# Decoding neighbour counts two per 16 bit word, with weights stored by parity of node

## The chip, the cores and the metric

The kernel runs on one core of a Trainium2 chip. The metric is the device time of the whole launch in microseconds (us). Before the change it is 418.17 us, the median of three runs (416.35 to 418.49). One further run was profiled; it is told of below.

## The reference

Two graph layers are computed over 3327 nodes with 64 features each and a symmetric 0/1 adjacency matrix `adj`. Layer 0 is attention in hyperbolic space: for every pair of nodes (i, j) with an edge, a sigmoid of two projections, times a logarithmic map of the pair, summed over j. Layer 1 is a weighted sum whose weights decay by rank:

```python
h = relu(layernorm(x));  x = x + layer0(h, adj)
h = relu(layernorm(x))
support = h @ weight
rank = cumsum(adj != 0, axis=1); deg = rank[:, -1:]; k = minimum(deg, 100.0)
pos = rank - (deg - k)
w = mask * where(pos > 0, 0.5 ** (k - pos), 0)
x = x + w @ support + bias
```

For a node i, the last neighbour in the order of j has the weight 1, the one before it 1/2, and so on, for at most 100 neighbours. So the weight of an edge (i, j) is fixed by how many neighbours of i stand behind j. That number, the count, fits in 8 bits. A 16 bit pattern that holds the count shifted left by seven places is, read as bf16, a power of two; the kernel uses this to turn counts into weights with a multiplication by 128.

## The kernel before, in words

The 3327 nodes are padded to 26 blocks of 128 (`NB`, 3328 columns, `NP`). The columns, which are the nodes i, are cut into four strips of 8, 8, 6 and 4 blocks (`STRIPS`). For each strip the blocks of nodes j (on the partitions) are walked from 25 down to 0 in rounds; a round holds up to 1024 columns.

In each round of the main loop (L1209) the adjacency tile comes by DMA (`ad`), ScalarE makes tanh (L653) and two Gelus (L857, L858) of products that TensorE has made (L670, L671), VectorE multiplies (L658, L663), and TensorE adds the result up over j (`po`, L680). Beside this, and for layer 1 only, VectorE makes a mask of the edges (L620), TensorE accumulates the counts in PSUM (`pc`, L631 and L632), and `read` takes the counts of one j out of PSUM with a clip at zero. It runs on ScalarE (L642) or VectorE (L644, L646); `ON_ACT` says in what share. 22 of the 26 blocks j are kept as 8 bit counts (`behind_lo`, `behind_hi`). Four blocks, `JD` = 12 to 15, are kept at once as 16 bit weights (`weight_of`), by a factor of 128 in the same read; there are 4 blocks by 4 strips = 16 such reads.

Layer 1 comes at the end. `order` lists the blocks j: first the four of `JD`, then 0 to 11 and 16 to 21; blocks 22 to 25 (`late`) come last, as their features are ready last. For each block that isn't in `JD`, `decode` turns its 3328 counts into a 16 bit tile `wt` of 3328 weights (7 buffers): the first, third and so on of the 22 on ScalarE (L1285), the others on VectorE (L1287). A decode is issued `LEAD` = 4 blocks ahead of its use. TensorE then adds seven products per block (L1299), one per chunk of 512 columns (the last has 256), into seven PSUM tiles `pw`.

Between the decodes stands another chain. The result of layer 0 for the last strip must pass through `post`: some forty operations on small tiles of VectorE (those that go through one helper all have the line L1044), three powers on GpSimd (also L1044), and three activations on ScalarE (L1086, L1136, L1147), until the features `s2` of the late blocks are there (L1149). The chain is cut in portions: each call of `advance` (L1311) puts at most 8 of them after a decode, and a step that waits for GpSimd costs two calls. The order on TensorE, VectorE and ScalarE is as written in the source (`IN_ORDER`), so a decode that waits for a buffer also holds the portions of `post` behind it. GpSimd also adds the bias to `x_sb` (L1304), ahead of the third power in its own queue.

When the features of the late blocks are there, TensorE goes chunk by chunk: four products of the late blocks, then a copy of the chunk from PSUM to SBUF (`ow`, L1340 on ScalarE, L1342 on VectorE), and later `close`: 128 columns at a time are multiplied by the weight matrix of layer 1 (L1328), `x_sb` is added (L1330), and the result goes out by DMA (L1332, L1334). `close` of a chunk comes after the late products of two further chunks.

Of the kernel before, what the change touches and what calls it, by code (L numbers as in the profile page):

```python
# [11 lines left out]
F32 = mybir.dt.float32  # L12
F16 = mybir.dt.float16
BF16 = mybir.dt.bfloat16
I32 = mybir.dt.int32
U16 = mybir.dt.uint16
U8 = mybir.dt.uint8
AF = mybir.ActivationFunctionType
ALU = mybir.AluOpType
# [3 lines left out]
P = 128  # L23
N = 3327
NB = 26
NP = NB * P
D = 64
# [3 lines left out]
JD = range(12, 16)  # L31
# [9 lines left out]
ROUND = (3.5, 3.5, 2.8, 1.9)  # L41

LEAD = 4

GSTRIPS = [(0, 7), (7, 7), (14, 6), (20, 6)]
GFMAX = 7 * P
# [35 lines left out]
def halves(n):  # L82
    return [(a, min(a + 512, n)) for a in range(0, n, 512)]
# [363 lines left out]
def fast(ctx, tc, x, adj_t, r, w_att, b_att, weight, bias, out, flag):  # L447

    nc = tc.nc
    V, A, G, T = nc.vector, nc.scalar, nc.gpsimd, nc.tensor  # L450
    const = ctx.enter_context(tc.tile_pool(name="f_const", bufs=1))

    x_sb = const.tile([P, NB, D], F32, name="x_sb")
# [14 lines left out]
    w2s = const.tile([P, D], F32, name="w2s")  # L468
# [67 lines left out]
    weight_of = const.tile([P, len(JD), NP], U16, name="weight_of")  # L536
    s2 = const.tile([P, NB, 2, D], F16, name="s2")
# [7 lines left out]
    def behind(j):  # L545
        if j in JD:
            return weight_of[:, j - JD.start]
        return behind_of["lo"][:, j] if j < JD.start else behind_hi[:, j - JD.stop]
# [53 lines left out]
    def span(n):  # L602
        k, lo, hi = rounds[n]
        return (hi - lo) * strips[k].F
# [17 lines left out]
    def count(n, j):  # L622
# [9 lines left out]
            T.matmul(S.pc[:, f0:f1], cb, now[:, f0:f1], start=S.first, stop=True, skip_group_check=True)  # L632
        S.before, S.first = now, False

    def read(n, j, on_act=None):
        k, lo, hi = rounds[n]
        S = strips[k]
        kept = behind(j)[:, S.i0 : S.i0 + S.F]
        num, den = ON_ACT[k]
        i = NB - 1 - j  # L640
        if on_act or (on_act is None and i * num // den != (i + 1) * num // den):
            A.activation(kept, S.pc[:, : S.F], AF.Relu, scale=128.0 if j in JD else 1.0)  # L642
        elif j in JD:
            V.tensor_scalar(kept, S.pc[:, : S.F], 0.0, 128.0, op0=ALU.max, op1=ALU.mult)  # L644
        else:
            V.tensor_scalar(kept, S.pc[:, : S.F], 0.0, None, op0=ALU.max)  # L646

# [58 lines left out]
    d, rl, sq, sr = (pre.tile([P, NB, D], F32, name=n) for n in ("d", "rl", "sq", "sr"))  # L706
# [3 lines left out]
    for hs in node_halves:  # L710
        n = hs.stop - hs.start
# [166 lines left out]
    for j in js(0):  # L878
        read(0, j, True)
# [10 lines left out]
    for b in (24, 20, 16, 12, 8, 4, 0):  # L890
        n = min(4, NB - b)
# [23 lines left out]
    for j in js(1):  # L915
        read(1, j, True)
# [267 lines left out]
    def advance(portions):  # L1184
        for stage in stages:
            while portions > 0 and not stage.asked:
                portion = next(stage.portions, LATER)
                stage.asked = portion == ACT
                if portion >= LATER:
                    break  # L1190
                portions -= portion

    def asked_of_act():
        for stage in stages:
            if stage.asked:
                next(stage.portions)
                stage.asked = False

    def finish():
        for stage in stages:  # L1200
            for _ in stage.portions:
                pass
        stages.clear()
# [5 lines left out]
    for n in range(2, R):  # L1209
        k, lo, hi = rounds[n]  # L1210
        m, w = n + AHEAD, span(n)
# [22 lines left out]
        if n == 2:  # L1234
            for j in js(2):
                read(2, j, True)
# [33 lines left out]

    late = STRIPS[-1][0]
    order = [*JD, *range(JD.start), *range(JD.stop, late)]
    chunks = halves(NP)
    with tc.tile_pool(name="l1", bufs=2, reuse_waits="tile") as l1, tc.manual_schedule(engines=IN_ORDER):
        decoded = 0

        def decode(j):

            nonlocal decoded
            if j in JD:  # L1280
                return behind(j)
            wt = l1.tile([P, NP], U16, name="wt", bufs=7)
            decoded += 1
            if decoded % 2:
                A.activation(wt, behind(j), AF.Copy, scale=128.0)  # L1285
            else:
                V.tensor_scalar(wt, behind(j), 128.0, None, op0=ALU.mult)  # L1287
            return wt

        every = [*order, *range(late, NB)]  # L1290
        weights = {j: decode(j) for j in every[: len(JD) + 1]}
        stages.append(Stage(per_node(len(STRIPS) - 1, pa)))
        sums.close()
        l1_ps = ctx.enter_context(tc.tile_pool(name="l1_ps", bufs=1, space=PSUM, reuse_waits="tile"))
        pw = [l1_ps.tile([P, f1 - f0], F32, name=f"pw{n}") for n, (f0, f1) in enumerate(chunks)]

        def add(j, wt, n):
            f0, f1 = chunks[n]
            T.matmul(pw[n], s2[:, j].rearrange("p c d -> p (c d)"), wt[:, f0:f1].bitcast(BF16),  # L1299
                     start=j == order[0], stop=j == NB - 1)  # L1300

        def bias(b0, nb):
            xb = x_sb[:, b0 : b0 + nb]
            G.tensor_add(xb, xb, bias_b[:, None, :].to_broadcast([P, nb, D]))  # L1304

        for i, j in enumerate(order):
            for jn in every[: i + 1 + LEAD]:
                if jn not in weights:
                    weights[jn] = decode(jn)
            asked_of_act()  # L1310
            advance(LAST)  # L1311
            for n in range(len(chunks)):
                add(j, weights[j], n)
            if i % 4 == 3 and i < STRIPS[-2][0]:
                bias(i - 3, 4)
        finish()
        bias(STRIPS[-2][0], late - STRIPS[-2][0])
        bias(late, NB - late)
        for j in range(late, NB):
            if j not in weights:  # L1320
                weights[j] = decode(j)
        ow = [l1.tile([P, 512], F32, name="ow", bufs=4)[:, : f1 - f0] for f0, f1 in chunks]

        def close(n):
            f0, f1 = chunks[n]
            b0, nb = f0 // P, (f1 - f0) // P
            for b in range(nb):
                T.matmul(pw[n][:, b * D : (b + 1) * D], ow[n][:, b * P : (b + 1) * P], w2s, start=True, stop=True)  # L1328
            o = l1.tile([P, 4, D], F32, name="o", bufs=4)
            V.tensor_add(o[:, :nb], pw[n][:, : nb * D].rearrange("p (b d) -> p b d", d=D), x_sb[:, b0 : b0 + nb])  # L1330
            full = nb if b0 + nb < NB else nb - 1
            nc.sync.dma_start(out[f0 : f0 + full * P, :].rearrange("(b p) d -> p b d", p=P), o[:, :full])  # L1332
            if full < nb:
                nc.scalar.dma_start(out[f0 + full * P : N, :], o[: N - f0 - full * P, full])  # L1334

        for n in range(len(chunks)):
            for j in range(late, NB):
                add(j, weights[j], n)
            if n % 2:
                A.copy(ow[n], pw[n])  # L1340
            else:
                V.tensor_copy(ow[n], pw[n])  # L1342
            if n > 1:
                close(n - 2)
        close(len(chunks) - 2)
        close(len(chunks) - 1)


@with_exitstack
def gnn_kernel(  # L1350
    ctx: ExitStack,
    tc: tile.TileContext,
    x: bass.AP,
    adj_t: bass.AP,
    r: bass.AP,
    w_att: bass.AP,
    b_att: bass.AP,
    weight: bass.AP,
    bias: bass.AP,
    out: bass.AP,  # L1360
):
    keep = ctx.enter_context(tc.tile_pool(name="keep", bufs=1))
    flag = keep.tile([1, 1], I32, name="flag")
    args = (x, adj_t, r, w_att, b_att, weight, bias, out)
    with ExitStack() as inner:
        fast(inner, tc, *args, flag)
    cond = tc.nc.values_load(flag)
    with tc.If(cond > 0):
        with ExitStack() as inner:
            general(inner, tc, *args)  # L1370
# [28 lines left out]
```

## Time and profile before

The profiled execution took 418.25 us by the device's own clock, and its span, from the first to the last instruction, is 416.4 us; 1.85 us lie outside the span. The median of the three runs shown, 418.17 us, stands 0.08 us below it.

| what | us |
|---|---|
| device time, profiled execution | 418.25 |
| its span | 416.4 |
| VectorE, ScalarE, TensorE busy | 373.1, 364.8, 361.1 |
| first product of layer 1 (L1299) starts | 360.26 |
| last product of the late blocks' first chunk starts | 396.89 |
| last VectorE sum ahead of the output (L1330) ends | 409.55 |
| 8 bit decode on ScalarE (L1285) | 11 of 2.96 |
| 8 bit decode on VectorE (L1287) | 11 of 1.89 |
| reads of the `JD` blocks on ScalarE (L642), on VectorE (L644) | 9 and 7 |

An instruction's duration in the trace covers its start and its end; on VectorE the next one starts some 75 ns before the end of the one in front, if it waits for nothing. The time from start to start of two neighbours is called the pitch here. "Granted clock" is the share of TensorE's full clock that it was given in a stretch.

### The profile page before, as it was taken

What the parts mean: (1) busy time and instruction counts of PE and PEld (TensorE: products, weight loads), DVE (VectorE), ACT (ScalarE), POOL (GpSimd) and SP (SyncE); (2) the same over time, 40 slices, a digit from 0 to 9 for tenths busy, and PEclk for the clock granted to TensorE, in tenths of its full rate; (3) what the DMA queues carried; (4) which work ended last, traced back from release to release, by engine and by line L of the source; (5) the groups of instructions that cost most, each with busy time, mean ns of one, the idle gap of its engine ahead of it and who ended that gap; (6) DMA issues with size and microseconds to landing.
All of it is one profiled execution on the core that took longest, in us unless ns stands there. A gap on an engine that the chain in (4) does not pass through costs nothing.

```text
span 416.4 us, 4699 instructions
## 1 busy us (share of the span) xinstructions
PE 361.1 (87%) x1436; PEld 154.4 (37%) x1460; DVE 373.1 (90%) x546; ACT 364.8 (88%) x411; POOL 124.0 (30%) x240
## 2 busy tenths in 40 slices
PE   0088999999997999999997999999777999899793
PEld 0063333333333333333333444444332333344352
DVE  4999799999999899999999798899989899898841
ACT  3589999999998899999999899999996999788810
POOL 8154200000000263930250163801405183452400
PEclk9998999999999899999999899999898999999987
DMA  7315544545466534554437255454643420000012
GB/s 218 123 40 143 161 148 147 158 145 161 146 186 181 152 107 148 153 151 109 145 113 178 94 153 151 119 146 128 186 117 104 114 87 0 2 0 0 2 25 65
DMA packets 23298, 48.99 MB, mean 118 GB/s; under 512 B 8789, under 2 KB 9245, under 8 KB 23265
## 3 DMA queue, kind: packets, MB, share of 16 engines
q1 hardware_dynamic: 20993, 47.66, 39.2%
q10 hardware_dynamic: 1808, 0.46, 0.6%
q0 software_dynamic: 464, 0.49, 0.5%
q8 instruction: 13, 0.21, 0.2%
q14 instruction: 20, 0.16, 0.1%
HBM read 46.40 MB, written 0.87 MB: 114 GB/s over the span
## 4 chain that ended last, share of the span: by engine, by line
DVE 33%; ACT 27%; PE 24%; issue 10%; POOL 3%; DMA 1%; DVEq 0%; POOLq 0%; ACTq 0%
DVE sg L663 9%; PE po L680 9%; ACT sg L653 8%; DVE sg L658 8%; ACT pq L857 8%; ACT pq L858 3%; DVE wt L1287 3%; PE pq L670 3%; PE pq L671 3%; DVE behind_lo L646 3%; PE pc L632 2%; PE pc L631 2%; ACT behind_lo L642 2%; ACT behind_hi L642 2%; PE pw L1299 2%
## 5 line engine op out<-in xcount | busy, mean ns | idle before, releaser
L680 PE MATMUL po<-sg,hw 128*65 128x512 f32 (+1 forms) x364 | 164.5, 576 | 0.5 <-DVE st L972 0.4
L663 DVE SCALAR_TENSOR_TENSOR sg<-pq,sg 128x1024 f32<-128x1024 f32 (+1 forms) x91 | 103.4, 1137 | 6.7 <-ACT pq L858 5.9
L658 DVE SCALAR_TENSOR_TENSOR sg<-sg,ad 128x1024 f32<-128x1024 f32 (+1 forms) x91 | 103.8, 1141 | 0.3
L653 ACT ACTIVATE sg<-left_b,right 128x1024 f32<-128x1024 f32 (+2 forms) x103 | 99.5, 979 | 0.0
L857 ACT ACTIVATE pq<-pq 128x1024 f32<-128x1024 f32 (+1 forms) x91 | 87.1, 957 | 3.5 <-PE pq L671 3.2
L858 ACT ACTIVATE pq<-pq 128x1024 f32<-128x1024 f32 (+1 forms) x91 | 86.2, 947 | 2.9
L680 PEld LDWEIGHTS po<-sg,hw 128*65 128x65 f32 x364 | 50.4, 141 | 71.3 <-issue 57.5
L631 PE MATMUL pc<-mask,ca 128*128 128x512 bf16 (+1 forms) x170 | 62.1, 365 | 11.1 <-DVE behind_hi L646 3.9
L670 PE MATMUL pq<-iu,ju 71*128 71x512 f16 (+1 forms) x182 | 68.2, 375 | 2.4 <-ACT jz L794 1.0
L671 PE MATMUL pq<-iz,jz 128*128 128x512 f16 (+1 forms) x182 | 67.2, 376 | 0.0
L632 PE MATMUL pc<-mask,cb 128*128 128x512 bf16 (+1 forms) x168 | 60.1, 368 | 2.2 <-ACT behind_lo L642 1.7
L620 DVE TENSOR_SCALAR mask<-ad 128x1024 bf16<-128x1024 f32 (+1 forms) x91 | 58.6, 645 | 0.0
L1044 POOL TENSOR_TENSOR dots<-dots,ih 128x8 f32<-128x8 f32 (+1 forms) x3 | 2.2, 720 | 134.3 <-DVE dots L1064 134.3
L1299 PE MATMUL pw<-wt,s 128*128 128x512 bf16 (+1 forms) x150 | 33.6, 374 | 4.3 <-DVE s L1149 2.2
L632 PEld LDWEIGHTS <-cb 128*128 128x128 bf16 x182 | 17.9, 98 | 51.7 <-issue 39.8
L631 PEld LDWEIGHTS <-ca 128*128 128x128 bf16 x175 | 17.3, 99 | 29.9 <-issue 17.8
L670 PEld LDWEIGHTS <-ju 71*128 71x128 f16 x182 | 18.1, 99 | 24.2 <-DVE sg L663 5.8
L1299 PEld LDWEIGHTS <-s 128*128 128x128 f16 x182 | 18.0, 100 | 23.6 <-issue 4.2
L642 ACT ACTIVATE behind_hi<-pc 128x1024 uint8<-128x1024 f32 (+2 forms) x25 | 21.8, 872 | 5.3 <-remote 3.3
L671 PEld LDWEIGHTS <-jz 128*128 128x128 f16 x182 | 18.2, 100 | 19.7 <-issue 3.3
L1304 POOL TENSOR_TENSOR x_sb<-x_sb,bias_b 128x256 f32<-128x256 f32 (+1 forms) x6 | 9.9, 1657 | 51.6 <-DVE w L1133 46.0
L642 ACT ACTIVATE behind_lo<-pc 128x1024 uint8<-128x1024 f32 (+2 forms) x29 | 24.9, 859 | 0.0
(313 smaller groups left out, 369.0 us busy)
## 6 DMA issues: line engine op xcount, KB each, us to landing
ad<-in_adj_t SPq DMA_DIRECT2D x65, 512.0 KB, 3.7
ad<-in_adj_t SPq DMA_DIRECT2D x26, 384.0 KB, 3.2
out<-o SPq DMA_DIRECT2D x6, 128.0 KB, 1.9
left_b<-left_d SPq DMA_DIRECT2D x1, 512.0 KB, 4.6
x_sb<-in_x ACTq DMA_DIRECT2D x1, 416.0 KB, 5.6
x_sb<-in_x SPq DMA_DIRECT2D x1, 416.0 KB
left_b<-left_d SPq DMA_DIRECT2D x1, 384.0 KB
jz<-iz POOLq DMA_DIRECT2D x2, 128.0 KB, 2.6
```

The costliest lines, as they stand in the source:

```text
L631: T.matmul(S.pc[:, f0:f1], ca, S.before[:, f0:f1], start=False, stop=True, skip_group_check=True)
L632: T.matmul(S.pc[:, f0:f1], cb, now[:, f0:f1], start=S.first, stop=True, skip_group_check=True)
L642: A.activation(kept, S.pc[:, : S.F], AF.Relu, scale=128.0 if j in JD else 1.0)
L653: A.activation(part(n, sg, j), S.left[:, : S.F], AF.Tanh, bias=right[:, j : j + 1], scale=0.5)
L658: V.scalar_tensor_tensor(sg, sg, 1.0, ad_of.pop(n)[:, :w], op0=ALU.add, op1=ALU.mult)
L663: V.scalar_tensor_tensor(sg, pq_of.pop(n)[:, :w], WD, sg, op0=ALU.add, op1=ALU.mult)
L670: T.matmul(part(n, pq, j, f0, f1), ju[:KB, j, :], S.iu[:, f0:f1], start=True, stop=False)
L671: T.matmul(part(n, pq, j, f0, f1), jz[:, j, :], S.iz[:, f0:f1], start=False, stop=True)
L680: T.matmul(S.po[: D + 1, f0:f1], hw[:, j, :], part(n, sg_of[n], j, f0, f1), start=j == NB - 1, stop=j == 0)
L857: A.activation(pq, pq, AF.Gelu, scale=-WG / QS)
L858: A.activation(pq, pq, AF.Gelu, scale=WH)
L1299: T.matmul(pw[n], s2[:, j].rearrange("p c d -> p (c d)"), wt[:, f0:f1].bitcast(BF16), start=j == order[0], stop=j == NB - 1)
```

## The change

Three things change.

A decode on VectorE now takes the 3328 counts of a block as 1664 words of 16 bits, with no conversion. One instruction masks the low byte of each word and shifts it left by 7; another masks the high byte and shifts it right by 1. The first gives the weights of the even nodes, the second those of the odd nodes, so a tile of weights is now stored by parity: 1664 even nodes, then 1664 odd ones. A decode on ScalarE reads the counts with a step of two to write the same order. Only every third decode now runs on ScalarE (`ACT_DECODES` = 3): 8 of the 22 on ScalarE, 14 on VectorE as 28 instructions.

The 16 reads of the `JD` blocks write this order too: they read PSUM with a step of two fp32 elements and write two contiguous runs.

The seven chunks of TensorE become three pairs (even and odd nodes of 1024 columns, 512 each) and one of 256, which reads two runs of 128. The copy from PSUM to SBUF puts the two chunks of a pair back in the order of the nodes, by writing with a step of two into one tile of 1024; VectorE copies the even chunk and the last one, ScalarE the odd chunk. `close` takes a pair at once, 8 blocks, after one further chunk's late products.

```diff
+ACT_DECODES = 3
...
+    def by_parity(t):
+        return t.rearrange("p (r k) -> p r k", r=2)
+
     def read(n, j, on_act=None):
...
+        of = S.pc[:, : S.F]
+        if j in JD:
+            kept = by_parity(weight_of[:, j - JD.start])[:, :, S.i0 // 2 : (S.i0 + S.F) // 2]
+            of = of.rearrange("p (k r) -> p r k", r=2)
         if on_act or (on_act is None and i * num // den != (i + 1) * num // den):
-            A.activation(kept, S.pc[:, : S.F], AF.Relu, scale=128.0 if j in JD else 1.0)
+            A.activation(kept, of, AF.Relu, scale=128.0 if j in JD else 1.0)
         elif j in JD:
-            V.tensor_scalar(kept, S.pc[:, : S.F], 0.0, 128.0, op0=ALU.max, op1=ALU.mult)
+            V.tensor_scalar(kept, of, 0.0, 128.0, op0=ALU.max, op1=ALU.mult)
...
-    chunks = halves(NP)
+    chunks = [(q, r) for q in range(3) for r in range(2)] + [(3, None)]
+    widths = [512] * 6 + [256]
...
-            if decoded % 2:
-                A.activation(wt, behind(j), AF.Copy, scale=128.0)
+            to = by_parity(wt)
+            if decoded % ACT_DECODES == 1:
+                A.activation(to, behind(j).rearrange("p (k r) -> p r k", r=2), AF.Copy, scale=128.0)
             else:
-                V.tensor_scalar(wt, behind(j), 128.0, None, op0=ALU.mult)
+                pairs_of = behind(j).bitcast(U16)
+                V.tensor_scalar(to[:, 0], pairs_of, 0xFF, 7, op0=ALU.bitwise_and, op1=ALU.logical_shift_left)
+                V.tensor_scalar(to[:, 1], pairs_of, 0xFF00, 1, op0=ALU.bitwise_and, op1=ALU.logical_shift_right)
...
-            T.matmul(pw[n], s2[:, j].rearrange("p c d -> p (c d)"), wt[:, f0:f1].bitcast(BF16),
+            q, r = chunks[n]
+            w = by_parity(wt.bitcast(BF16))[:, :, 512 * q : min(512 * q + 512, NP // 2)]
+            T.matmul(pw[n], s2[:, j].rearrange("p c d -> p (c d)"), w if r is None else w[:, r],
                      start=j == order[0], stop=j == NB - 1)
...
+        def copied(n):
+            q, r = chunks[n]
+            to = kept_of[q].rearrange("p (k r) -> p r k", r=2)
+            if r is None:
+                V.tensor_copy(to, by_parity(pw[n]))
+            elif r == 0:
+                V.tensor_copy(to[:, 0], pw[n])
+            else:
+                A.copy(to[:, 1], pw[n])
...
+        def close(q):
+            for h in range(0, 8 if q < 3 else 2, 4):
+                b0 = 8 * q + h
+                nb = min(4, NB - b0)
+                pc = pw[2 * q + h // 4]
+                for b in range(nb):
+                    T.matmul(pc[:, b * D : (b + 1) * D], kept_of[q][:, (h + b) * P : (h + b + 1) * P], w2s, start=True, stop=True)
...
         for n in range(len(chunks)):
             for j in range(late, NB):
                 add(j, weights[j], n)
-            if n % 2:
-                A.copy(ow[n], pw[n])
-            else:
-                V.tensor_copy(ow[n], pw[n])
-            if n > 1:
-                close(n - 2)
-        close(len(chunks) - 2)
-        close(len(chunks) - 1)
+            copied(n)
+            if n > 0 and n % 2 == 0:
+                close(n // 2 - 1)
+        close(3)
```

More of the change, by code (lines that the diff above doesn't have):

```diff
@@ L1294, in fast @@
         l1_ps = ctx.enter_context(tc.tile_pool(name="l1_ps", bufs=1, space=PSUM, reuse_waits="tile"))
-        pw = [l1_ps.tile([P, f1 - f0], F32, name=f"pw{n}") for n, (f0, f1) in enumerate(chunks)]
+        pw = [l1_ps.tile([P, f], F32, name=f"pw{n}") for n, f in enumerate(widths)]
         def add(j, wt, n):
-            f0, f1 = chunks[n]
-            T.matmul(pw[n], s2[:, j].rearrange("p c d -> p (c d)"), wt[:, f0:f1].bitcast(BF16),
+            q, r = chunks[n]
+            w = by_parity(wt.bitcast(BF16))[:, :, 512 * q : min(512 * q + 512, NP // 2)]
+            T.matmul(pw[n], s2[:, j].rearrange("p c d -> p (c d)"), w if r is None else w[:, r],
                      start=j == order[0], stop=j == NB - 1)
@@ L1321, in fast @@
                 weights[j] = decode(j)
[L1322 to L1334, printed above, removed]
+        kept_of = [l1.tile([P, min(NP - 1024 * q, 1024)], F32, name="ow" if q < 3 else "ow_last", bufs=2 if q < 3 else 1)
+                   for q in range(4)]
+        def copied(n):
[14 more added lines that the diff above has]
+                    T.matmul(pc[:, b * D : (b + 1) * D], kept_of[q][:, (h + b) * P : (h + b + 1) * P], w2s, start=True, stop=True)
+                o = l1.tile([P, 4, D], F32, name="o", bufs=4)
+                V.tensor_add(o[:, :nb], pc[:, : nb * D].rearrange("p (b d) -> p b d", d=D), x_sb[:, b0 : b0 + nb])
+                full = nb if b0 + nb < NB else nb - 1
+                f0 = b0 * P
+                nc.sync.dma_start(out[f0 : f0 + full * P, :].rearrange("(b p) d -> p b d", p=P), o[:, :full])
+                if full < nb:
+                    nc.scalar.dma_start(out[f0 + full * P : N, :], o[: N - f0 - full * P, full])
         for n in range(len(chunks)):
```

## The prediction, on record before the result was known

> **What bounds the kernel now.** I read the page's first two parts, then a table of stretches, then the engines' timelines of the end of the kernel, then the rows of the changed lines.
>
> ```profile
> span 416.4 us, 4699 instructions
> ...
> 66.00:84.00 18.00, 17.72 (x61) 6.63 (x61) 18.00 (x19) 17.34 (x19) 0.00 (x0) 1.00 0.55 157
> ...
> 360.30:396.90 36.60, 32.22 (x156) 15.22 (x158) 33.07 (x74) 30.54 (x15) 15.58 (x11) 1.00 0.00 1
> 396.90:400.40 3.50, 3.50 (x11) 1.62 (x11) 0.69 (x2) 0.59 (x1) 0.00 (x0) 0.58 0.00 0
> ```
>
> The columns are the stretch, its length, the busy time of TensorE, its weight loads, VectorE, ScalarE and GpSimd, then granted clock, DMA share, GB/s. In the main loop (66 to 84, where four `JD` blocks of strip 0 are read) VectorE has no free moment and ScalarE 0.66 us. In the decode stage (360.3 to 396.9) none is full. What ends last there is seen on TensorE's timeline (start, duration, then what it is; in brackets the wait ahead of it):
>
> ```profile
> 360.26 5.78 PE L1299 MATMUL pw<-weight_of,s 128*128 128x512 bf16 x27
> 365.88 18.42 PE L1299 MATMUL pw<-wt,s 128*128 128x512 bf16 x89
> 385.37 7.53 PE L1299 MATMUL pw<-wt,s 128*128 128x512 bf16 x34 [1.08 <-DVE wt L1287]
> 395.10 0.60 PE L1299 MATMUL pw<-wt,s 128*128 128x512 bf16 x2 [2.19 <-DVE s L1149]
> 396.27 0.38 PE L1299 MATMUL pw<-wt,s 128*128 128x512 bf16 x1 [0.57 <-ACT wt L1285]
> 396.89 3.47 PE L1299 MATMUL pw<-wt,s 128*128 128x512 bf16 x9 [0.25 <-DVE wt L1287]
> ```
>
> TensorE runs without a break to 384.3, at 1.4 us for a block (six products at 0.216 us, one at 0.108), waits 1.08 us for a decode, ends the 22 early blocks at 392.9, waits 2.19 us for the late features (L1149, at 395.0), then for the last two decodes. Had it never waited, the early blocks would have ended at 360.26 + 22 x 1.4 = 391.1. After the long wait it runs at a clock of 0.58: nine products take 3.47 us, 0.386 each. So the stage is bound by VectorE's order: the `post` chain with 1.89 us decodes between its steps.
>
> ```profile
> 378.38 1.88 DVE L1287 TENSOR_SCALAR wt<-behind_lo 128x3328 uint16<-128x3328 uint8 x1
> 381.16 0.16 DVE L1044 TENSOR_TENSOR rt_last<-rn_last 128x4 f32<-128x4 f32 x1 [0.90 <-POOL rn_last L1044]
> ...
> 378.55 2.58 POOL L1044 TENSOR_TENSOR rn_last<-y_last,nhalf 128x4 f32<-128x4 f32 x1 [8.43 <-DVE y_last L1044]
> ```
>
> The power on GpSimd shows 2.58 us, but ends 0.87 us after the decode beside it (378.38 + 1.88 = 380.26); the third power does the same (0.88 us after its decode). The decode holds it up.
>
> **What the Trainium skill says.** "VectorE: DVE Perf Modes", section "The perf-mode tier table": `tensor_scalar` in SBUF handles two elements a cycle, and four where both sides have 2-byte types. The trace agrees for two: 3328 counts in 1.885 us, 1664 cycles of 0.96 GHz plus 0.15 us. It has no large 2-byte case. Nor does the page say that bit operations have these modes. The trace speaks for it: a shift and a multiply-add of one shape take the same 190 ns.
>
> ```profile
> 14.31 0.19 DVE L512 TENSOR_SCALAR t<-v 128x52 int32<-128x52 int32 x1
> 14.54 0.19 DVE L513 TENSOR_SCALAR y<-t 128x52 int32<-128x52 int32 x1
> ```
>
> One element a cycle would make them 54 ns longer than their 4-element kin (0.16 to 0.17 us); they are some 25 ns longer.
>
> "SBUF — State Buffer", section "Who interferes with whom": VectorE in a two-port mode and GpSimd exclude each other for a whole instruction. The held power above agrees as far as GpSimd goes; no decode was held by GpSimd (all 11 take 1.88 to 1.90 us).
>
> "PSUM — Partial Sum Buffer", section "Specifications (TRN2)": lines of 8 bytes, and a pattern that isn't contiguous slows matmuls. What a step of 8 bytes costs ScalarE or VectorE isn't said, and no row here shows it.
>
> **The change part by part.** All sums are against the profiled execution, 418.25 us (span 416.4 and 1.85 outside; the median of the runs is 0.08 lower).
>
> 1. *Decode on VectorE.* Half a decode is 1664 words, an estimate from that tier table and the 0.15 us of the old decode: at four a cycle 433 + 152 = 585 ns, pitch 0.51; a pair 1.02 against a pitch of 1.82. Two a cycle: 1.02 us, pitch 0.94, a pair 1.87. One a cycle: 1.885, a pair 3.62. I take four. 14 pairs are 14.3 us, for 11 x 1.82 = 20.0.
>
> 2. *Decode on ScalarE.* Three fewer: 3 x 2.87 = 8.6 us less. The step of two bytes I price at nothing. It can't gain; up to 8.6 / 8 = 1.07 us each is hidden by the time set free.
>
> 3. *What the pairs do to the order.* I walk VectorE's new order with the old durations. The `post` steps stay; pairs stand where VectorE's decodes stood, with three more. To 361.59 nothing changes. Two pairs, two sums and the first 11 small steps (1.61) bring the first `t_last` to 365.9 (before 367.5). GpSimd's chain for strip 2, which lost 1.5 us to one decode (a step of 0.25 took 1.72 at 365.36), ends near 366, not 367.7; its power ends by 368.5. VectorE: two pairs and the strip 2 features to 368.9; five steps (1.08) to 370.0, a pair to 371.0 that hides the tanh; eight steps (1.5), a pair, twelve steps (1.75) to 375.3; two pairs to 377.4, under which the second power is held and then ends 0.9 later, 378.2. Six small steps, three wide ones, two pairs and three wide ones to 383.9; ScalarE's square and the sum after it to 384.9. Then GpSimd's bias (1.57) and third power stand beside two pairs (to 387.0) and end at 387.9; four steps and a wide one to 389.0. A pair to 390.0, the cast under it, L1149 to 390.4, the last pair to 391.4. No pair waits for its buffer: the twentieth decode needs the thirteenth block's products, done at 360.26 + 17 x 1.4 = 384.1. The last decode, on ScalarE, stands behind the cast (389.5): 2.97 more, 392.5. The fourth product of the first late chunk, which needs it, starts at 392.5 and not 396.89: -4.4.
>
> 4. *Clock.* Waits of TensorE fall to 0.7 us or less ahead of that product. A wait of 1.08 us left the clock at 1.00 in the trace. So nine products cost 9 x 0.216 = 1.94 for 3.47, and the first `close` 0.84 for 1.15: -1.8.
>
> 5. *End.* The products are the same in number; ten blocks' `close` stand after the last late product in both orders. What is new: `close` of the third pair needs ScalarE's copy of chunk 5 (0.59 us and some 0.3 of signals), hidden only by chunk 6 (0.44): +0.45, and some 0.05 at the first pair. Copies that write with a step of two I price as before (0.69 and 0.59); up to 0.3 us more each would show three times: +0.9 at worst. Together +0.5. The DMAs after L1330 are as before, and no queue is passed.
>
> 6. *Reads of `JD`.* 9 on ScalarE (7424 columns, 6.2 us of streaming at the row's rate) and 7 on VectorE (5888, 6.1 us; 1.21 us for 1024) read PSUM with a step of two. I take no cost: both write one element a cycle at most as it is, and the lines follow each other in order. Nothing hides a cost there (VectorE 18.00 of 18.00 busy). The other bound is a price of the skill for SBUF ("Vector Engine (DVE) Microarchitecture Reference", section 5.2, "Measured stream behaviour on trn2"): hopping each element on one source 1.73 ns against 1.054, small steps 2.5. As an estimate that is +7.9 us at 1.64 times, +17 at 2.4. It can't gain. In the instruction order two of ScalarE's reads in strip 3 also wait for VectorE now, with the two Gelus queued behind them. I price that at nothing: `pc` is one tile, so TensorE makes the count that they read only after VectorE has read the one before.
>
> Sum: -4.4 - 1.8 + 0.5 = -5.7, so 418.25 - 5.7 = 412.5.
>
> **Rivals.**
>
> *Strided reads cost what the skill has for SBUF.* For it: each read takes one element of an 8-byte line. Against: the page names matmuls only. 412.5 + 7.9 = 420.4. It undoes the gain from 5.7 / 12.3 = 0.46 of the streaming time upward.
>
> *Bit operations don't get four a cycle (the case that ends slower).* Place: VectorE between 361.59 and L1149. At a pair of 1.87: 14 x 1.87 = 26.2, other work 13.1 (35.2 from 361.59 to 396.8, less 20.0 of decodes and 2.0 idle), waits 1.9: the last decode ends at 402.8, 6.0 later, and the end adds 0.5: 424.7. It decides from a pair of 1.44 us, 0.72 per half. At one element a cycle 14 x 3.62 puts it 30.5 later, near 449. Against it: the two 190 ns rows.
>
> *The stage doesn't follow.* If the power waits out more than the pairs, or the clock still drops, 3 to 4 us of the 6.2 go: about 416.5.
>
> **How the numbers follow.** About 0.5% (2.1 us) can be told from no change: below 416.1 is faster, above 420.3 slower. Forecast 0.54 (411 to 416); strided reads 0.27 (0.04 faster, 0.09 same, 0.14 slower); two a cycle 0.11, one a cycle 0.03, both slower; not following 0.05, same. Faster 0.58, same 0.14, slower 0.28. The likeliest is 412.5. Range: below, no exposed copy and the walk 0.7 us earlier gives 411. Above, 422 leaves out both bit cases (0.14) and the dear end of the strided reads (0.05).
>
> **What would show it.** Right: halves of L1298 and L1299 at some 585 ns; the `weight_of` rows still 1.01 and 1.21 us; L1157 ending near 390; no wait of TensorE over 1.1 us and a clock of 1.00 from 390 to 404; the last L1356 near 404. Wrong: halves of 1.0 us or more, `weight_of` reads above 1.4 and 1.7 us, or the main loop ending later than 357.

## The result and the profile after

The changed kernel takes 411.03 us (median of 4 runs, 410.35 to 412.49); the kernel before, run beside it, takes 417.26 (4 runs, 415.86 to 418.49). The ratio is 0.9845, with a 95% interval of 0.9801 to 0.9889: 6.5 us less by the ratio, between 4.6 and 8.3. Later runs say the same: 410.86 for the changed kernel (6 runs) beside 416.42 for the one before (11 runs), a ratio of 0.9858 [0.9822, 0.9894].

The first view is the page's head, the stretch of the main loop that the prediction read (66 to 84), and the decode stage. As layer 1's first product starts at 357.97 here and not at 360.26, the decode stage is taken from 357.97 on, over the same 36.6 us. The columns are those of the prediction.

```profile
span 408.6 us, 4737 instructions
...
66.00:84.00 18.00, 17.94 (x63) 6.68 (x62) 18.00 (x20) 17.33 (x19) 0.00 (x0) 1.00 0.55 154
...
357.97:394.57 36.60, 36.60 (x191) 18.58 (x190) 29.36 (x95) 22.98 (x14) 8.34 (x11) 1.00 0.02 5
```

In this stretch of the main loop nothing has moved: VectorE is full, ScalarE at 17.33 of 18.00. In the decode stage VectorE fell from 33.07 to 29.36, ScalarE from 30.54 to 22.98, GpSimd from 15.58 to 8.34, and TensorE, which had been idle for 4.4 us there, is full. On TensorE's timeline, from the first product of layer 1:

```profile
357.97 5.78 PE L1312 MATMUL pw<-weight_of,s 128*128 128x512 bf16 x28
363.59 28.03 PE L1312 MATMUL pw<-wt,s 128*128 128x512 bf16 x138
391.47 2.00 PE L1354 MATMUL pw<-w2s,ow 128*128 128x64 f32 x16
393.30 1.89 PE L1312 MATMUL pw<-wt,s 128*128 128x512 bf16 x8
395.04 2.00 PE L1354 MATMUL pw<-w2s,ow 128*128 128x64 f32 x16
396.87 1.46 PE L1312 MATMUL pw<-wt,s 128*128 128x512 bf16 x8
398.64 2.00 PE L1354 MATMUL pw<-w2s,ow 128*128 128x64 f32 x16 [0.31 <-ACT ow L1346]
400.48 0.61 PE L1354 MATMUL pw<-w2s,ow_last 128*128 128x64 f32 x4
```

Four waits (1.08, 2.19, 0.57 and 0.25 us before) are gone: the early blocks outside `JD` and the late products of the first three chunks run as one row of 28.03 us. One wait is new, for ScalarE's copy of the last odd chunk (L1346). With no wait, the fourth late product of chunk 0 starts three products after the 22 early blocks: at 389.51 in the trace, 31.54 us after the first product (22 x 1.4 + 3 x 0.216 gives 31.45).

The rows of the changed operations, by form (duration min/median/max in ns, then first and last start):

```profile
L1298 DVE TENSOR_SCALAR wt<-behind_lo x8: 576/584/594, 359.3 to 374.0; 128x1664 uint16<-128x1664 uint16 x8
L1299 DVE TENSOR_SCALAR wt<-behind_lo x8: 575/582/587, 359.8 to 374.5; 128x1664 uint16<-128x1664 uint16 x8
...
L1295 ACT ACTIVATE wt<-behind_lo x4: 2960/2965/2971, 352.5 to 368.6; 128x3328 uint16<-128x3328 uint8 x4
```

A half takes 584 ns. That is the prediction's estimate for four words a cycle, 585 ns. ScalarE's decode with a source step of two bytes still takes 2.96 us.

### The profile page after: what moved, and what is told of

Same layout as the page of the kernel before. It is cut to its first block, busy times and chain, and to the rows that moved or that the text cites. A ratio compares the mean times of both kernels' runs of the same rounds, so it can differ in the third digit from the quotient of the medians.

```text
span 408.6 us, 4737 instructions
## 1 busy us (share of the span) xinstructions
PE 356.6 (87%) x1460; PEld 152.1 (37%) x1460; DVE 367.2 (90%) x563; ACT 356.1 (87%) x408; POOL 116.7 (29%) x240
## 4 chain that ended last, share of the span: by engine, by line
DVE 34%; ACT 30%; PE 22%; issue 11%; DMA 1%; DVEq 0%; ACTq 0%
DVE sg L671 12%; DVE sg L666 10%; PE pw L1312 9%; ACT sg L661 9%; ACT pq L865 8%; PE po L688 4%; ACT pq L866 4%; DVE behind_lo L654 3%; ACT behind_hi L650 2%; DVE behind_hi L654 2%; ACT behind_lo L650 2%; PE pq L678 2%; PE pq L679 2%; PE pw L1354 2%; PE pc L632 1%
## 5 line engine op out<-in xcount | busy, mean ns | idle before, releaser
L688 PE MATMUL po<-sg,hw 128*65 128x512 f32 (+1 forms) x364 | 161.2, 566 | 0.4 <-DVE st L980 0.4
L632 PE MATMUL pc<-mask,ca 128*128 128x512 bf16 (+1 forms) x175 | 63.9, 365 | 12.9 <-DVE behind_hi L654 4.7
L688 PEld LDWEIGHTS po<-sg,hw 128*65 128x65 f32 x364 | 49.2, 138 | 69.2 <-issue 55.0
L633 PE MATMUL pc<-mask,cb 128*128 128x512 bf16 (+1 forms) x182 | 64.9, 367 | 1.8 <-ACT behind_lo L650 1.7
L679 PE MATMUL pq<-iz,jz 128*128 128x512 f16 (+1 forms) x182 | 66.0, 370 | 0.0
L1052 POOL TENSOR_TENSOR dots<-dots,ih 128x8 f32<-128x8 f32 (+1 forms) x3 | 2.2, 720 | 131.6 <-DVE dots L1072 131.6
L1312 PE MATMUL pw<-wt,s 128*128 128x512 bf16 (+1 forms) x154 | 31.4, 364 | 0.0
L679 PEld LDWEIGHTS <-jz 128*128 128x128 f16 x182 | 18.1, 99 | 19.1 <-issue 2.3
L1317 POOL TENSOR_TENSOR x_sb<-x_sb,bias_b 128x256 f32<-128x256 f32 (+1 forms) x6 | 8.3, 1393 | 52.0 <-DVE w L1141 46.0
```

Source lines behind the costliest of these rows:

```text
L632: T.matmul(S.pc[:, f0:f1], ca, S.before[:, f0:f1], start=False, stop=True, skip_group_check=True)
L679: T.matmul(part(n, pq, j, f0, f1), jz[:, j, :], S.iz[:, f0:f1], start=False, stop=True)
L688: T.matmul(S.po[: D + 1, f0:f1], hw[:, j, :], part(n, sg_of[n], j, f0, f1), start=j == NB - 1, stop=j == 0)
L1312: T.matmul(pw[n], s2[:, j].rearrange("p c d -> p (c d)"), w if r is None else w[:, r], start=j == order[0], stop=j == NB - 1)
```

## Where the time went: three stretches

Layer 1's first product divides the kernel in two, and the product just named divides the rest. The first columns are the profiled executions of both kernels; the last is `after_again`, the changed kernel run once more (expectation below).

| stretch, us | before | after | difference | after_again |
|---|---|---|---|---|
| up to the first product of layer 1 | 360.26 | 357.97 | -2.3 | 360.29 |
| from there to the fourth late product of chunk 0 | 36.63 | 31.54 | -5.1 | 31.54 |
| from there to the end of the span | 19.51 | 19.09 | -0.4 | 19.17 |
| span | 416.4 | 408.6 | -7.8 | 411.0 |

The lower two rows are the change's own: -5.5 us. The upper row is the main loop, and needs a look at the granted clock. Two stretches just after a turn from one strip to the next, in the kernel before:

```profile
132.00:138.00 6.00, 4.90 (x18) 2.27 (x20) 5.66 (x8) 5.56 (x8) 0.00 (x0) 0.72 0.42 132
228.00:234.00 6.00, 5.36 (x22) 2.77 (x23) 5.40 (x8) 5.93 (x10) 0.00 (x0) 0.72 0.43 127
```

the changed kernel:

```profile
132.00:138.00 6.00, 4.73 (x22) 2.11 (x23) 5.66 (x8) 5.33 (x8) 0.00 (x0) 1.00 0.39 119
228.00:234.00 6.00, 6.00 (x31) 3.00 (x30) 5.61 (x9) 5.94 (x10) 0.00 (x0) 1.00 0.40 105
```

and the changed kernel once more:

```profile
132.00:138.00 6.00, 4.90 (x18) 2.29 (x20) 5.65 (x8) 5.56 (x8) 0.00 (x0) 0.72 0.38 125
228.00:234.00 6.00, 5.33 (x22) 2.74 (x23) 5.43 (x8) 5.91 (x11) 0.00 (x0) 0.72 0.42 127
```

Read the third number from the right. Where the changed kernel's clock falls at the same turns, its main loop ends at 360.29, against 360.26 before. So the 2.3 us are not the edit's: the same program shows both ends, and the earlier one goes with a clock that stayed up. The comparison of profiles with like main loops is 418.25 with 412.73 (`after_again`), 5.5 us.

> The changed kernel once more with a profile. My theory: 410.5 to 412.5; its first product of layer 1 starts where the granted clock at the strip turns puts it, 358 to 361, and TensorE has no wait from there to the seventh chunk.

> The kernel before, once more with a profile. My theory (the main loop of the changed kernel ended 2.3 us earlier by chance of the granted clock at the strip turns, not by the change): its time is as before, 415.9 to 418.5, and its first product of layer 1 starts anywhere between 357.9 and 361. Rival (the change shortens the main loop): it starts near 360.3 again, and the changed kernels all near 358.

The kernel before, run again, took 418.17 (22 runs, all but one between 414.66 and 420.40) beside 416.51 for the 45 other runs of the same program on that chip: the same program gives medians 1.7 us apart and single runs nearly 6 us apart. Its first product of layer 1 starts at 361.86, 0.9 us later than the latest that I had expected. Below, "stage" is the time from the first product of layer 1 to the end of the span, which leaves most of this spread out: 56.1 and 55.6 in the two profiles of the kernel before, 50.6 and 50.7 in the two of the changed one, so the change is worth 4.9 to 5.5 us there. The 0.5 us between the two profiles of the kernel before lie behind TensorE's last product, where the last sums and the output's DMA took 7.2 and 6.7 us.

## The experiments

The theory is that the word decode shortens VectorE's order, so that TensorE no longer waits; the clock then stays up; the new layout costs a little at the end, and the strided reads nothing. The rivals are these: the relief of ScalarE is what counts; the layout is; the reads cost something, or gain something.

### Layout and end alone (e_layout)

The changed kernel with the old decode, one ScalarE decode in two:

```diff
-ACT_DECODES = 3
+ACT_DECODES = 2
...
-                pairs_of = behind(j).bitcast(U16)
-                V.tensor_scalar(to[:, 0], pairs_of, 0xFF, 7, op0=ALU.bitwise_and, op1=ALU.logical_shift_left)
-                V.tensor_scalar(to[:, 1], pairs_of, 0xFF00, 1, op0=ALU.bitwise_and, op1=ALU.logical_shift_right)
+                V.tensor_scalar(to, behind(j).rearrange("p (k r) -> p r k", r=2), 128.0, None, op0=ALU.mult)
```

> The changed kernel with the old arithmetic of the decode: VectorE takes 8 bit counts with a step of two and multiplies by 128, one instruction for a block, every second decode on ScalarE as before. The layout by parity, the reads of the kept blocks and the new end stay. My theory (all of the gain is the faster decode): the decodes stay at 1.89 us, TensorE waits for the late features as before, and the time is that of the kernel before plus 0.5 for the end, 417.8. Rival (the layout and the order of the end bring the gain): 414 or less.

Measured: 418.53 against 416.51, ratio 1.0046 [1.0022, 1.0071]; stage 57.4. TensorE's timeline of this run:

```profile
383.65 7.53 PE L1310 MATMUL pw<-wt,s 128*128 128x512 bf16 x34 [1.10 <-DVE wt L1297]
393.38 0.60 PE L1310 MATMUL pw<-wt,s 128*128 128x512 bf16 x2 [2.19 <-DVE s L1157]
394.55 0.38 PE L1310 MATMUL pw<-wt,s 128*128 128x512 bf16 x1 [0.57 <-ACT wt L1295]
395.18 3.40 PE L1310 MATMUL pw<-wt,s 128*128 128x512 bf16 x9 [0.25 <-DVE wt L1297]
```

The four waits of the kernel before are all back, within 0.02 us, with the slow products behind them. So the layout brings nothing by itself; it costs. From the product at 395.18 to the end are 20.7 us, for 19.5 before: +1.2, more than the prediction's +0.5. (Up to TensorE's last product it is +0.8.) The median is 0.7 above my 417.8.

### The old decode in the new share (e_share)

```diff
-                pairs_of = behind(j).bitcast(U16)
-                V.tensor_scalar(to[:, 0], pairs_of, 0xFF, 7, op0=ALU.bitwise_and, op1=ALU.logical_shift_left)
-                V.tensor_scalar(to[:, 1], pairs_of, 0xFF00, 1, op0=ALU.bitwise_and, op1=ALU.logical_shift_right)
+                V.tensor_scalar(to, behind(j).rearrange("p (k r) -> p r k", r=2), 128.0, None, op0=ALU.mult)
```

> The changed kernel with the old arithmetic of the decode (8 bit counts with a step of two, times 128, one instruction for a block), and one decode of three on ScalarE, 14 on VectorE. My theory: VectorE's order gets 3 x 1.82 = 5.5 us longer than with 11, no gain in return, 422 to 423.5. Rival (what helps is to relieve ScalarE): 417 or less.

Measured: 422.01 against 416.42, 1.0133 [1.0092, 1.0174]; stage 61.8. Taking three decodes off ScalarE costs 4.4 us of stage beyond `e_layout` while VectorE decodes bytes at 1.885 us.

### The new decode in the old share (e_half)

```diff
-ACT_DECODES = 3
+ACT_DECODES = 2
```

> The changed kernel with every second decode on ScalarE, 11 there and 11 pairs of bit instructions on VectorE; nothing else differs. My theory (the pairs shorten VectorE's order and TensorE becomes the bound, with ScalarE only just full): 0.3 to 1.2 us above the changed kernel, 411.3 to 412.2; the last ScalarE decode ends near 388 to 390. Rival (the gain is that ScalarE was relieved of three decodes): 414 or more.

Measured: 410.64 against 416.51, 0.9885 [0.9846, 0.9923]; stage 50.9. I had expected a loss against the changed kernel, and there is none that can be measured (410.86 for that): ScalarE's last decode ends at 388.93, 30.9 us after the first product, and TensorE needs its weights only with the third late product, which starts at 389.39, after 31.3. So with the word decode ScalarE's share is worth nothing. The four stages of this layout put the whole gain on the word decode of VectorE: with every second decode on ScalarE it takes 57.4 to 50.9 (`e_layout`, `e_half`), with every third 61.8 to 50.6 (`e_share`, the changed kernel).

### Words, but written in the order of the nodes (e_order)

The kernel before with the word decode and the new share; each half writes every second word, so layout, reads and end are the old ones:

```diff
-            if decoded % 2:
+            if decoded % 3 == 1:
...
-                V.tensor_scalar(wt, behind(j), 128.0, None, op0=ALU.mult)
+                pairs_of = behind(j).bitcast(U16)
+                to = wt.rearrange("p (k r) -> p r k", r=2)
+                V.tensor_scalar(to[:, 0], pairs_of, 0xFF, 7, op0=ALU.bitwise_and, op1=ALU.logical_shift_left)
+                V.tensor_scalar(to[:, 1], pairs_of, 0xFF00, 1, op0=ALU.bitwise_and, op1=ALU.logical_shift_right)
```

> The kernel before with the decode by 16 bit words and one decode of three on ScalarE, but without the layout by parity: the two bit instructions write every second 16 bit element of the tile, in the order of the nodes. Reads of the kept blocks, chunks and end are those of before. It sets the rate of the prediction's rival by hand. My theory (a written step of two costs the mode of four a cycle): halves of about 1.02 us at two a cycle, VectorE's order 6 us longer than before, 424 to 425. At one a cycle halves of 1.885 us and near 449. Rival (the step doesn't matter): halves of 585 ns, the changed kernel's time less 0.5 us, 410.5.

```profile
L1289 DVE TENSOR_SCALAR wt<-behind_lo x8: 1083/1100/1114, 363.5 to 384.9; 128x1664 uint16<-128x1664 uint16 x8
L1290 DVE TENSOR_SCALAR wt<-behind_lo x8: 1079/1094/1108, 364.5 to 385.9; 128x1664 uint16<-128x1664 uint16 x8
```

Measured: 423.97 against 416.42, 1.0154 [1.011, 1.0199]; stage 61.2. A step of two on the writing side takes a half from 584 to 1100 ns. Two such halves take 1.98 us from start to start, more than one old decode (1.82). This is what the layout by parity is for. It is also the prediction's rival of two words a cycle, priced there at 1.02 us for a half and 424.7 in all.

### The strided reads alone (e_reads)

The kernel before with only the `JD` reads by parity. It leaves out the rest of the layout, so layer 1's sum pairs these weights with the wrong nodes; the amount of work is the same.

```diff
+        of = S.pc[:, : S.F]
+        if j in JD:
+            kept = by_parity(weight_of[:, j - JD.start])[:, :, S.i0 // 2 : (S.i0 + S.F) // 2]
+            of = of.rearrange("p (k r) -> p r k", r=2)
...
-            A.activation(kept, S.pc[:, : S.F], AF.Relu, scale=128.0 if j in JD else 1.0)
+            A.activation(kept, of, AF.Relu, scale=128.0 if j in JD else 1.0)
...
-            V.tensor_scalar(kept, S.pc[:, : S.F], 0.0, 128.0, op0=ALU.max, op1=ALU.mult)
+            V.tensor_scalar(kept, of, 0.0, 128.0, op0=ALU.max, op1=ALU.mult)
```

> The kernel before, with one part of the change alone: the sixteen reads of the kept weights from PSUM (L650 on ScalarE, L652 on VectorE) take every second element, and write run by run; the decode is the old one. The kept blocks' weights then stand in parity order while the rest of layer 1 is in node order, so part of layer 1's sum pairs weights with the wrong nodes; the amount of work is that of the kernel before. Theory (a step of two between fp32 elements of PSUM costs these reads nothing): each read stays at about 1.01 us on ScalarE and 1.21 us on VectorE, and the time stays at that of the kernel before, 416.5, within 1. Rival of the prediction (reads at half rate): ScalarE's go to about 2.0 us and VectorE's to 2.3 us, and the time goes to 420 or above. Second rival (the reads are what made the changed kernel's main loop end 2.3 us earlier): about 414.5.

```profile
L649 ACT ACTIVATE weight_of<-pc x9: 583/802/1014, 71.3 to 329.5; 128x1024 uint16<-128x1024 f32 x4, 128x768 uint16<-128x768 f32 x3, 128x512 uint16<-128x512 f32 x2
L651 DVE TENSOR_SCALAR weight_of<-pc x7: 677/1216/1225, 68.5 to 327.7; 128x1024 uint16<-128x1024 f32 x4, 128x512 uint16<-128x512 f32 x2, 128x768 uint16<-128x768 f32 x1
```

In the kernel before:

```profile
L642 ACT ACTIVATE weight_of<-pc x9: 583/801/1015, 71.5 to 329.7; 128x1024 uint16<-128x1024 f32 x4, 128x768 uint16<-128x768 f32 x3, 128x512 uint16<-128x512 f32 x2
L644 DVE TENSOR_SCALAR weight_of<-pc x7: 679/1212/1224, 68.7 to 327.9; 128x1024 uint16<-128x1024 f32 x4, 128x512 uint16<-128x512 f32 x2, 128x768 uint16<-128x768 f32 x1
```

Measured: 416.74 against 416.56, 1.0015 [0.9992, 1.0037]. The rows are the same within 4 ns. The first product of layer 1 starts at 360.10. The reads cost nothing that can be measured, and they gain nothing.

### TensorE kept busy in its long wait (e_fill)

The kernel before with nine products that nobody needs, in the place of the 2.19 us wait:

```diff
+        spare = l1_ps.tile([P, 512], F32, name="spare")
...
+        for _ in range(9):
+            T.matmul(spare, s2[:, 0].rearrange("p c d -> p (c d)"), weight_of[:, 0, :512].bitcast(BF16), start=True, stop=True)
```

> The kernel before, with TensorE kept busy: nine more 128x512 products on blocks that are there already, into a PSUM tile that nothing reads, issued after the early blocks of chunk 0, where TensorE waited 2.19 us for the late features. Nothing else is changed; the decode is the old one. Theory (the late products at 0.386 us in the kernel before are slow because the granted clock falls after that wait): the late products take about 0.216 us, the end comes 1.5 to 1.8 us sooner than in the kernel before, so 414.7 to 415.0 where that has 416.5. The stretch from the first product of layer 1 to the end of the span goes from 56 us to 54 to 54.5. Rival (the slow products are due to something else, such as the order of the pools or the ends that the profile models): they stay at 0.386 us, and the time stays at 416.5 or goes up by up to 0.5.

```profile
391.80 2.11 PE L1318 MATMUL spare<-weight_of,s 128*128 128x512 bf16 x9
394.15 0.61 PE L1300 MATMUL pw<-wt,s 128*128 128x512 bf16 x2 [0.25 <-DVE s L1149]
395.32 0.38 PE L1300 MATMUL pw<-wt,s 128*128 128x512 bf16 x1 [0.57 <-ACT wt L1285]
395.95 2.10 PE L1300 MATMUL pw<-wt,s 128*128 128x512 bf16 x9 [0.25 <-DVE wt L1287]
```

Measured: 415.19 against 416.56, 0.9968 [0.9947, 0.9988]; stage 54.7, so both lie 0.2 above what I had expected. More work on TensorE makes the kernel 1.4 us faster. The nine late products take 2.10 us and not 3.47; from the last line's start to the end are 18.05 us, for 19.51. So the clock term is real: -1.5 us in the stage, with no decode changed. Up to TensorE's last product it is -1.7 (10.65 us for 12.33). The Trainium skill ("TensorE: Matmul & The Clock Gate", section "HAM oscillation — how this bites in real kernels") warns of idle gaps of over about 3.4 us; here one of 2.19 us, followed by two short ones, was enough, and one of 1.08 us was not.

The length of the waits doesn't settle it. Ahead of the late products, `e_share` and `e_order` wait about as long:

```profile
396.65 0.60 PE L1310 MATMUL pw<-wt,s 128*128 128x512 bf16 x2 [1.87 <-DVE s L1157]
398.44 4.00 PE L1310 MATMUL pw<-wt,s 128*128 128x512 bf16 x10 [1.19 <-DVE wt L1297]
```

```profile
403.12 0.60 PE L1302 MATMUL pw<-wt,s 128*128 128x512 bf16 x2 [2.02 <-DVE s L1149]
405.10 2.32 PE L1302 MATMUL pw<-wt,s 128*128 128x512 bf16 x10 [1.38 <-DVE wt L1290]
```

In `e_share` (the first two rows) ten products then take 4.00 us, at a granted clock of 0.56; in `e_order` 2.32 us, at 1.00. What decides between the two isn't shown here.

### Closing one chunk later (e_close), and both (e_both)

The changed kernel; `close` of a pair comes after two further chunks' late products, as in the kernel before, and `e_both` has one ScalarE decode in two beside it:

```diff
-            if n > 0 and n % 2 == 0:
-                close(n // 2 - 1)
+            if n in (3, 5):
+                close((n - 3) // 2)
+        close(2)
         close(3)
```

> The changed kernel with the first two groups of closing products one chunk later (after the fourth and the sixth chunk's late products), so that the copy of the sixth chunk on ScalarE lies under eight closing blocks. My theory: the one wait of TensorE of 0.31 us ahead of the third group goes, and nothing else moves: 0.3 us less than the changed kernel. Rival (the end is set by what comes after TensorE, the sums and the DMAs): no change, or a little more because the first output leaves 0.9 us later.

> The changed kernel with the groups of layer 2 closed one chunk later, as in e_close, and with one decode in two on ScalarE, as in e_half. Theory (TensorE sets the end, from its first product of layer 1 on, once it never waits for the late features): ScalarE's relief is worth nothing, so the time is that of e_close, 409.6 within 0.6, and the stretch from the first product to the end of the span is 49.6 within 0.5. Rival (the copies of sums on ScalarE still hold TensorE back at the end, and ScalarE's decodes are what makes them late): 408.5 or less. Second rival (VectorE gets back work that delays the late features): 410.5 or more, with a wait on TensorE ahead of the late products.

TensorE's timeline of `e_close`, from the second row on:

```profile
364.98 28.89 PE L1312 MATMUL pw<-wt,s 128*128 128x512 bf16 x139
393.71 1.89 PE L1354 MATMUL pw<-w2s,ow 128*128 128x64 f32 x16
395.44 1.89 PE L1312 MATMUL pw<-wt,s 128*128 128x512 bf16 x8
397.17 1.90 PE L1354 MATMUL pw<-w2s,ow 128*128 128x64 f32 x16
398.90 0.60 PE L1312 MATMUL pw<-wt,s 128*128 128x256 bf16 x4
399.33 1.90 PE L1354 MATMUL pw<-w2s,ow 128*128 128x64 f32 x16
401.07 0.61 PE L1354 MATMUL pw<-w2s,ow_last 128*128 128x64 f32 x4
```

The wait for L1346 is gone, and each group of sixteen small products takes 1.89 or 1.90 and not 2.00 us: there had been a short wait inside each. From the fourth late product (31.54 us after the first one, at 390.90) to the end are 18.1 us, for 19.1 in the changed kernel: about 1 us, where I had expected 0.3. The stage is 49.6. The median is 409.60 (6 runs), its ratio to the kernel before 0.9838 [0.9807, 0.987]; `e_both` has 410.56 (6 runs), 0.9859 [0.9825, 0.9893], and a stage of 49.7. The median of `e_both` is 1.0 above the 409.6 that I had expected within 0.6, and so falls where the second rival had it, but without that rival's wait of TensorE; its stage is as expected. Closing later shows in both traces as 1 us; the intervals of the medians are too wide to separate either from the changed kernel. The two have the shortest stages seen.

## Why the prediction's number was wrong, and what of it held

By its own steps, with the profile's numbers:

| step | predicted | measured | from |
|---|---|---|---|
| 1, a half on VectorE | 585 ns | 584 ns | rows of L1298, L1299 |
| 2, a decode on ScalarE | as before | 2.96 us, as before | row of L1295 |
| 3, the order up to the fourth late product | -4.4 | -5.1 | 36.63 to 31.54 |
| 4, the clock | -1.8 | -1.5 | `e_fill`, 19.51 to 18.05 |
| 5, the end | +0.5 | +1.0 | 18.05 to 19.09; `e_layout` +1.2 |
| 6, the reads of `JD` | 0 | 0 | `e_reads` |
| sum | -5.7 | -5.5 | stage, 56.14 to 50.63 |

The step that failed is the starting time of the sum, and with it the low end of the range. The prediction set its -5.7 us against one profiled execution of 418.25 us, which agreed with a median of three runs. The 99 runs of the kernel before that stand beside the experiments have medians of 416.4 to 416.6 (only the 22 runs of `before_again` give 418.17). From 416.5 the same -5.7 reads 410.8, and the changed kernel takes 410.86. The low end, 411, was for "no exposed copy and the walk 0.7 us earlier" (412.5 less 0.5 and 0.7 is 411.3). It had room for errors in the stage and none for the main loop, which step 6 priced at no change and which moves by 2 us between executions with the clock at the strips' turns. The median, 411.03, lies on that edge, and the ratio applied to the runs beside it (0.9845 x 417.26 = 410.8) just below it. A range below the forecast as wide as the kernel's own runs are spread would have held it.

In the stage the mechanism held: TensorE no longer waits, and its clock stays up. That the stage's sum came within 0.2 us was luck, as two errors cancel (with the second profile of the kernel before, -4.9, it is 0.8). Up to TensorE's last product alone, steps 4 and 5 are -1.7 and +0.9; the 6.7 to 7.6 us behind it, in the profiles compared here, blur the figures of the table by some tenths.

Step 3 was mis-sized on GpSimd. The walk let the second and third power wait until all the halves beside them were done and then take 0.87 us more, as they had with one long decode. GpSimd and then VectorE in the changed kernel:

```profile
373.21 1.46 POOL L1052 TENSOR_TENSOR rn_last<-y_last,nhalf 128x4 f32<-128x4 f32 x1 [8.09 <-DVE y_last L1052]
380.60 0.73 POOL L1317 TENSOR_TENSOR x_sb<-x_sb,bias_b 128x256 f32<-128x256 f32 x1 [5.93 <-DVE w_last L1141]
381.70 1.46 POOL L1052 TENSOR_TENSOR rn_last<-t_last,nhalf 128x4 f32<-128x4 f32 x1 [0.38 <-DVE t_last L1052]
```

```profile
373.04 0.58 DVE L1298 TENSOR_SCALAR wt<-behind_lo 128x1664 uint16<-128x1664 uint16 x1
373.54 0.58 DVE L1299 TENSOR_SCALAR wt<-behind_lo 128x1664 uint16<-128x1664 uint16 x1
374.05 0.58 DVE L1298 TENSOR_SCALAR wt<-behind_lo 128x1664 uint16<-128x1664 uint16 x1
374.55 0.58 DVE L1299 TENSOR_SCALAR wt<-behind_lo 128x1664 uint16<-128x1664 uint16 x1
375.05 0.15 DVE L1052 TENSOR_TENSOR rt_last<-rn_last 128x4 f32<-128x4 f32 x1
```

The second power ends at 374.67, inside the fourth half and not 0.87 us after it, and L1052 follows at once; the third does the same. Twice 0.87 are 1.7 us. The bias stands beside no half, as it is done before the next pair starts, and takes 0.73 us and not 1.57. So the late features come earlier than the walk had them: L1157 ends at 386.09, 28.1 us after the first product, where the walk gave 390.4 - 360.26 = 30.1. ScalarE's last decode ends at 388.07, 30.1 us after it (walk: 32.24). Both are then early enough for TensorE never to wait, and the 31.54 us of TensorE's own products take over as the bound. That is why only 0.7 of the 2 us show in step 3.

Step 5 was too small. The wait that it named is there (0.31 us where it is shown), but all three pairs' `close` wait some for ScalarE's copies, and the gaps around them add up to 0.8 us on TensorE, which `e_close` gives back.

Of the rivals, two words a cycle is a real price (`e_order`), but belongs to writing with a step; the strided reads have no price that shows; the stage did follow. The 2.5 ns of the dear end stand in section 5.2, which the prediction cites, for steps on both sources or on the destination alone, so for one source they were a guess. One sum of the prediction is slightly off: 48 elements more at one a cycle are 50 ns, not 54; the reading of the two 190 ns rows stays.

One thing stays open. In the stretch from 228 to 234 the clock fell in all five profiles of kernels with the old layout in layer 1, `e_reads` among them (0.72 to 0.85), and in one of seven with the new one (1.00 in the other six). The medians leave little for it: the changed kernel's gain of 5.6 us (410.86 from 416.42) is the stage's 4.9 to 5.5 and hardly more. An estimate says the same: the median span less the stage puts the first product of layer 1 at 358.4 to 358.9 in the kernel before (414.5 for those 99 runs) and at 358.5 in the changed one (409.15 for 10 runs). So a typical main loop ends no later in the kernel before; its profiled executions were late ones. Whether the changed program makes the fall less likely was not tried by itself.

## What to carry to other kernels

Before you split a long conversion into cheaper pieces, find which engine's order it sits in: here three fewer decodes on ScalarE were worth nothing beside the word decode, and 14 short ones between the steps of a chain on VectorE were worth 5 us; GpSimd's powers beside them also ended sooner. A wait of TensorE can cost twice, where the clock falls behind it, so price the products after the wait too. And set a forecast against the median of many runs, with a range no narrower than the spread of the same program.

## What the runs showed of the hardware

- How long VectorE holds GpSimd up depends on what stands in a row on VectorE. The same power of 128x4 took 2.58 us beside one decode of 1.89 (`e_layout`), 3.56 beside two in a row (`e_share`), 3.91 across four halves of 1.09 (`e_order`), but 1.46 beside four halves of 0.58 (the changed kernel), where it ended inside the fourth. A read that is let in at the next gap between two instructions, 0.87 us of work, and a write that is let in at the gap after that would fit the first two and the last. It doesn't fit `e_order`, where the power should then have ended near 385.0 and ended at 387.01, 0.04 us after the last of the four halves. So the rule stays open. The rows of `e_share` and `e_order` are shown below this list.
- It goes the other way as well. In `e_half` a half that should take 0.58 us took 1.11 (379.01 to 380.12) beside GpSimd's bias (378.67 to 379.68). The Trainium skill ("SBUF — State Buffer", section "Who interferes with whom") calls it an exclusive lock; the prediction had seen VectorE hold GpSimd only.
- A step of two on a 16 bit output nearly doubles the time of the VectorE instruction (1664 words, 584 to 1100 ns); on an fp32 source in PSUM it costs VectorE and ScalarE nothing that can be measured (1216 ns for 1212, 1014 for 1015).
- The clock after a strip's turn is 0.72 in one execution and 1.00 in another of the same program, and the end of the main loop differs by 2.3 us between the two. After waits of like length ahead of the late products it is 0.56 in `e_share` and 1.00 in `e_order`.

In `e_share`, GpSimd:

```profile
377.80 3.56 POOL L1052 TENSOR_TENSOR rn_last<-y_last,nhalf 128x4 f32<-128x4 f32 x1 [8.50 <-DVE y_last L1052]
```

and VectorE beside it:

```profile
377.63 3.69 DVE L1297 TENSOR_SCALAR wt<-behind_lo 128x3328 uint16<-128x3328 uint8 x2
```

The power starts 0.17 us into the first decode and ends at 381.36, 0.04 us after the second.

In `e_order`, GpSimd, and the last of the four halves beside it:

```profile
383.10 3.91 POOL L1044 TENSOR_TENSOR rn_last<-y_last,nhalf 128x4 f32<-128x4 f32 x1 [11.22 <-DVE y_last L1044]
385.89 1.08 DVE L1290 TENSOR_SCALAR wt<-behind_lo 128x1664 uint16<-128x1664 uint16 x1
```
